# The first layer's last convolution on two row halves of TensorE, x pieces kept in SBUF, stores moved to GpSimd's queue, and an earlier start of the second scan chunk

## The chip, the cores and the metric

The kernel runs on 1 core of one Trainium2 chip. The metric is the device time of one execution in microseconds (us). The kernel before was run three times: 11592.89 us is the median, from 11590.45 to 11595.39. The engines are named as in the profile: PE (TensorE), DVE (VectorE), ACT (ScalarE), POOL (GpSimd) and SP (SyncE, which here only issues DMAs).

## The reference

Two pre-activation layers with residuals on x of shape (4, 192, 128, 128), all in float32:

```python
x = x + _L0_conv_ref(_gn(x), ...)   # layer0 in the code
x = x + _L1_conv_ref(_gn(x), ...)   # layer1 in the code: the selective scan
```

`_gn` is a group norm over 32 groups of 6 channels. The first layer, cut to what matters:

```python
x1 = c1x1(gn(x), conv1_w)                    # 192 -> 48 channels: x_0, x_05, x_1, 16 each
Fre = frft2d(x_05, 0.5)                      # fractional Fourier transform
mag_out, pha_out = ...                       # 3x3 and 1x1 convolutions on |Fre| and angle(Fre)
ifrft = abs(frft2d(mag_out * exp(1j*pha_out), -0.5))
fre = rfft2(x_1)                             # the same with an ordinary 2D FFT and a 1x1 convolution
x_1o = irfft2(...)
y = c1x1(concat([c1x1(x_0, conv_0_w) + conv_0_b, ifrft, x_1o]), conv2_w)   # 48 -> 192 channels
```

The second layer turns each image into 16384 tokens of 192 channels, applies a layer norm, an input projection to 2 x 384, a causal convolution of 4 taps and SiLU, forms dt, B and C, runs the recurrence `h = h * exp(dt*A) + dt*u*B` with 16 states for each of 384 channels, gates `sum(h*C) + u*D` with SiLU(z) and projects back to 192 channels.

## The kernel before, in words

**`layer0`** takes the four images one after another. An image is cut into 16 pieces of 8 rows: a piece (tile `xt`) is 96 partitions x 2 x 1024 floats, 768 KB, loaded by `load` (L186, SP's queue) into a pool of 6 buffers. Three generators do the work of an image.

- `analysis` reads all 16 pieces for the group statistics (`bn`, L192, DVE), folds them into the weights `w1r`, and reads all 16 pieces a second time for the first convolution (L278). L278 works on two column halves of PE: output channels of the first 512 pixels go to PSUM partitions 0 to 63, those of the second 512 to 64 to 127. ACT evacuates (L282) and stores the 48 channels into the DRAM tensor `d1` (L288, ACT's queue).
- `branches` (26 steps) loads `d1`'s upper 32 channels (L294), does the two-sided transforms as matmuls (`spectrum`, L214 and L224), turns them into magnitude and phase (`_polar`: DVE, ACT, and one POOL add at L78), and passes every change of layout through DRAM: stores of `dmag`, `dp` (L303), `dh` (L310), `df` (L372), `di` (L392), `dimg` (L453) and loads of the same, all on SP's queue. The squares of the inverse transform are added on POOL (L421).
- `synthesis` is the last convolution with the residual. Per piece it loads `xt` again, 16 channels of `d1`, 32 of `dimg` and a row of ones into `cat` (49 rows x 1024; L464, L465, L466, SP's queue, two buffers), multiplies the 49 rows by `w2x` (L471: four matmuls of 49 rows, 96 columns and 512 elements), adds the result to `xt` (L475, DVE), takes the statistics for the second layer (L192) and stores the piece into `xmid` (L477, POOL's queue, software descriptors).

At L488 to L497 the generators are interleaved: each step of `branches(b)` is followed by one or two steps of `analysis(b + 1)` (`ahead`) and, at even steps, by one of `synthesis(b - 1)` (`behind`); what is left of both is run out before the next image. `synthesis(3)`, of the last image, runs alone. Within `layer0` a planner with assumed costs decides the order of instructions on each engine; an engine's order is then fixed, and an instruction that waits holds back all that follow on its engine or queue.

**`layer1`** has 128 chunks of 512 tokens; its order is written out by hand. `front(n)` is a generator of 34 steps for what comes ahead of the scan: layer norm (L610 to L658), input projection (L664), convolution (L682), SiLU (L690, L694), x projection (L726), the store of B and C to DRAM (`dbc`, L731), dt (L740, L745), dtu (L749, POOL) and the rest of the projection. `load_bc` broadcasts a pair of states' B and C from `dbc` to 128 partitions (`bc`, 1 MB each, 8 per chunk, L774). The main loop has 24 groups (3 channel tiles x 8 pairs of states) per chunk: scans on DVE (L869) with factors from ACT (L800) and inputs from DVE (L820), POOL (L828) or PE (L855), products with C on POOL (L882), sums on PE (L895). Steps of `front(n + 1)` and `front(n + 2)` run within the loop. Before the loop `front(0)` runs to its end, then the eight `load_bc` of chunk 0 and the first factors are issued, and then 10 steps of `front(1)`.

Of the kernel before, what the change touches and what calls it, by code (L numbers as in the profile page):

```python
# [121 lines left out]
def layer0(tc, x, xmid, st2, w):  # L122

    nc = tc.nc
    B = x.shape[0]
    with ExitStack() as ctx:
        def pool(name, bufs, **kw):
            return ctx.enter_context(tc.tile_pool(name=name, bufs=bufs, **kw))

        cp = pool("l0c", 1)  # L130
        dram = pool("l0d", 2, space=DRAM)
        xp = pool("l0x", 6)
        sp = pool("l0s", 2)
        imp = pool("l0i", 2)
        zp = pool("l0z", 2)
# [13 lines left out]
        ri_cat, ri_out = const("ri_cat"), const("ri_out")  # L149


        w2x = cp.tile([3 * NC + 1, C], F32, name="w2x")
        nc.sync.dma_start(out=w2x[NC : 3 * NC, :], in_=w["w2T"][NC:, :])
        w20, c0 = cp.tile([NC, C], F32, name="w20"), const("c0")
        nc.sync.dma_start(out=w20, in_=w["w2T"][0:NC, :])
        ps = psA.tile([128, 512], F32, name="ps")
        nc.tensor.matmul(ps[0 : NC + 1, 0:C], c0, w20, start=True, stop=True)
        folded = cp.tile([NC + 1, C], F32, name="folded")
        nc.vector.tensor_copy(folded, ps[0 : NC + 1, 0:C])
        nc.sync.dma_start(out=w2x[0:NC, :], in_=folded[0:NC, :])  # L160
        nc.sync.dma_start(out=w2x[3 * NC :, :], in_=folded[NC:, :])
        half_pi = cp.tile([128, 1], F32, name="half_pi")
        nc.vector.memset(half_pi, math.pi / 2)

# [4 lines left out]
        dmag = []  # L169
        zrow = cp.tile([1, S], F32, name="zrow")  # L170
        nc.vector.memset(zrow, 0.0)
        orow = cp.tile([1, PIECE], F32, name="orow")
        nc.vector.memset(orow, 1.0)
        for i in range(min(2, B)):
            d = dram.tile([NC * S + 2, S], F32, name=f"dmag{i}", bufs=1)
            nc.sync.dma_start(out=d[0:1, :], in_=zrow)
# [6 lines left out]
        def load(b, p):  # L183
            xt = xp.tile([CH, 2, PIECE], F32, name="xt")
            src = x[b].rearrange("c h w -> c (h w)")[:, p * PIECE : (p + 1) * PIECE]
            nc.sync.dma_start(out=xt, in_=split(src))  # L186
            return xt

        def bn(st, p, xt):
            for t in range(2):  # L190
                for q in range(PIECE // 512):
                    nc.vector.bn_stats(  # L192
                        st[:, t, p * (PIECE // 512) + q, :], xt[:, t, q * 512 : (q + 1) * 512]
                    )
# [52 lines left out]
        def analysis(b, got):  # L247


            st = sp.tile([CH, 2, NPIECE * (PIECE // 512), 6], F32, name="st")  # L250
            for p in range(NPIECE):
                bn(st, p, load(b, p))
                yield
            gst = sp.tile([CH, 2, 2], F32, name="gst")
            bn_done(st, gst)

            w1r = sp.tile([CH, 2, 128], F32, name="w1r")
            for t in range(2):  # L260
                nc.vector.tensor_scalar(w1r[:, t, :], w1T[:, t, :], gst[:, t, 1:2], None, ALU.mult)
            ps = psA.tile([128, 512], F32, name="ps")
            for t in range(2):
                nc.tensor.matmul(
                    ps[:, 0:1], w1r[:, t, :], gst[:, t, 0:1], start=t == 0, stop=t == 1
                )
            b1 = sp.tile([128, 1], F32, name="b1")
            nc.vector.tensor_scalar(b1, ps[:, 0:1], -1.0, None, ALU.mult)
            d1 = got["d1"] = dram.tile([3 * NC, S * S], F32, name="d1")
            for p in range(NPIECE):  # L270
                xt = load(b, p)
                if p % 2 == 0:
                    x1 = sp.tile([128, 2, 512], F32, name="x1")
                ps = psA.tile([128, 512], F32, name="ps")
                for t in range(2):
                    for q in range(2):
                        half = slice(64 * q, 64 * (q + 1))
                        nc.tensor.matmul(  # L278
                            ps[half], w1r[:, t, half], xt[:, t, q * 512 : (q + 1) * 512],
                            start=t == 0, stop=t == 1,  # L280
                        )
                nc.scalar.activation(x1[:, p % 2, :], ps, AF.Identity, bias=b1)  # L282
                if p % 2 == 1:
                    at = d1[:, (p - 1) * PIECE : (p + 1) * PIECE].rearrange(
                        "c (e q f) -> q c e f", e=2, q=2
                    )
                    for q in range(2):
                        nc.scalar.dma_start(out=at[q], in_=x1[64 * q : 64 * q + 3 * NC])  # L288
                yield

        def branches(b, got):
# [6 lines left out]
            for half in range(2):  # L298
                mag, pha = yield from spectrum(
                    xT, 0, fr2[:, 0, :], fr2, S, (2 * half, 2 * half + 1)  # L300
                )
                for src, dst in ((mag, dm[1 : NC * S + 1, :]), (pha, dp)):
                    nc.sync.dma_start(  # L303
                        out=by_row(dst, 8 * half, 8), in_=src.rearrange("k (c l) -> k c l", c=8)
                    )

            dh = [dram.tile([NC * S, L], F32, name=f"dh{i}") for i in range(2)]
            polar = yield from spectrum(xT, NC, rf1, rf2, L, range(4))
            for src, dst in zip(polar, dh):
                nc.sync.dma_start(  # L310
                    out=by_row(dst, 0, NC), in_=src.rearrange("k (c l) -> k c l", c=NC)
                )

# [20 lines left out]
            for half in range(2):  # L334
# [34 lines left out]
                    )  # L369
                    yield  # L370
                for src, dst in zip(_from_polar(nc, up, half_pi, mo, po, n), df):
                    nc.sync.dma_start(  # L372
                        out=dst.rearrange("(p r) l -> p (r l)", r=16)[:, half * n : (half + 1) * n],
                        in_=src,
                    )
# [13 lines left out]
                inner.append(t)  # L389
                yield  # L390
            for src, dst in zip(_from_polar(nc, up, half_pi, *inner, n), di):
                nc.sync.dma_start(out=dst.rearrange("(p r) l -> p (r l)", r=16), in_=src)  # L392


            img = imp.tile([128, 2 * NC, S], F32, name="img")
# [54 lines left out]
                )  # L450
                yield
            dimg = dram.tile([2 * NC, S, S], F32, name="dimg")
            nc.sync.dma_start(out=dimg.rearrange("c h w -> h c w"), in_=img)  # L453
            got.update(dimg=dimg)

        def synthesis(b, got):

            d1, dimg = got["d1"], got["dimg"].rearrange("c h w -> c (h w)")
            st = sp.tile([CH, 2, NPIECE * (PIECE // 512), 6], F32, name="st2")
            for p in range(NPIECE):  # L460
                xt = load(b, p)
                cat = qp.tile([3 * NC + 1, PIECE], F32, name="cat", bufs=2)
                at = slice(p * PIECE, (p + 1) * PIECE)
                nc.sync.dma_start(out=cat[0:NC, :], in_=d1[0:NC, at])  # L464
                nc.sync.dma_start(out=cat[NC : 3 * NC, :], in_=dimg[:, at])  # L465
                nc.sync.dma_start(out=cat[3 * NC :, :], in_=orow)  # L466
                for q in range(PIECE // 512):
                    at = slice(q * 512, (q + 1) * 512)
                    pr = psB.tile([128, 2, 512], F32, name="pr")
                    for t in range(2):  # L470
                        nc.tensor.matmul(  # L471
                            pr[0:CH, t, :], w2x[:, t * CH : (t + 1) * CH], cat[:, at],
                            start=True, stop=True,
                        )
                    nc.vector.tensor_add(xt[:, :, at], xt[:, :, at], pr[0:CH])  # L475
                bn(st, p, xt)
                nc.gpsimd.dma_start(  # L477
                    out=split(xmid[b][:, p * PIECE : (p + 1) * PIECE]), in_=xt
                )
                yield  # L480
            bn_done(st, st2[:, b])
# [6 lines left out]
        behind = iter(())  # L488
        for b in range(B):
            ahead = analysis(b + 1, got[b + 1]) if b + 1 < B else iter(())  # L490
            for i, _ in enumerate(branches(b, got[b])):
                next(ahead, None)
                next(ahead if i % 2 else behind, None)
            for rest in (behind, ahead):
                for _ in rest:
                    pass
            behind = synthesis(b, got[b])  # L497
        for _ in behind:
            pass

# [3 lines left out]
def layer1(tc, xmid, out, st2, w, n_tok=S * S):  # L504
# [12 lines left out]
    with ExitStack() as ctx:  # L517
# [253 lines left out]
        def load_bc(i, sg):  # L771

            t = bcp.tile([128, 2, G, T], F32, name="bc")
            nc.sync.dma_start(  # L774
                out=t, in_=got[i]["dbc"][:, sg * G : (sg + 1) * G, :].partition_broadcast(128)
            )
            got[i]["bc", sg] = t
# [184 lines left out]
        def go_on(parts, part):  # L962

            for f in parts[part]:
                got_on = next(f, None)
                if got_on is not None:
                    parts[got_on].append(f)

        with tc.manual_schedule():
            for i in range(min(2, total)):  # L970
                load_x(i)
            for _ in front(0):
                pass
            for sg in range(NG):
                load_bc(0, sg)
            dtu_copy(0, 0)
            inputs(*order[1])
            for at in range(AHEAD):
# [3 lines left out]
            decay_there(2)  # L982


            start_front(1)
            for _ in range(NGR - FRONT):
                parts = {MID: [], LATE: []}
                step(fronts, parts)
                go_on(parts, MID)
                go_on(parts, LATE)  # L990
            tails = []
            for pos, (n, k) in enumerate(order):
                j, sg = divmod(k, NG)
# [193 lines left out]
```

## Time and profile before

| | before |
|---|---|
| median of 3 runs | 11592.89 us |
| the profiled execution | 11590.68 us |
| its span, first to last instruction | 11588.6 us |
| granted PE clock, mean | 0.931 |
| DVE, POOL, PE, ACT busy | 93%, 87%, 85%, 74% of the span |
| `layer0`, to the last statistics (L192) | 0 to 1440 us |
| before the first scan (L869) | 1440 to 1523 us |
| scans | 1523 to 11588 us |

The span is what the profiler saw; the 2.1 us beside it lie around it. In a timeline line the first number is the start in us from the span's start, the second the duration; in brackets stands how long the engine had been idle and what released it. "x8" counts records, and each of these float32 matmuls leaves two. In a table by windows each engine has its busy time and the number of records, then follow the granted PE clock as a fraction, the mean busy share of the 16 DMA engines and GB/s.

### The profile page before, as it was taken

The numbers are of one execution on the slowest core, as the hardware profiler recorded it, in microseconds if no ns is written. First come the engines' busy times: TensorE is split into PE (matmuls) and PEld (weight loads), VectorE is DVE, ScalarE is ACT, GpSimd is POOL, SyncE is SP. The second block draws the span as 40 slices with busy tenths as digits, with TensorE's granted clock in tenths as the row PEclk, the third lists the DMA queues.
The fourth block names the chain that finished last, engine by engine and source line by source line (L and its number), as shares of the span: only waits on it lengthen the run. The fifth ranks groups of instructions, "written<-read, shape, count | busy, mean of one in ns | idle before, by whom it ended". The sixth has DMA issues, their size and how long they took to land.

```text
span 11588.6 us, 153548 instructions
## 1 busy us (share of the span) xinstructions
PE 9794.3 (85%) x50570; PEld 6612.4 (57%) x50570; DVE 10751.8 (93%) x11584; ACT 8608.4 (74%) x14436; POOL 10072.1 (87%) x4598
## 2 busy tenths in 40 slices
PE   4777888888888888888888888888888888888887
PEld 2444356655656665655665665665655666566565
DVE  5565679999999999999999999999999999999999
ACT  2322168888888888888888888888888888888886
POOL 0000079999999999999999999999999999999999
PEclk8888789999999999999999999999999999999998
DMA  8787734434434434433433443443443343344343
GB/s 209 203 221 202 195 99 126 120 108 127 126 103 128 126 107 122 126 112 117 126 118 110 126 125 104 127 127 104 124 126 111 118 126 116 113 126 123 106 127 97
DMA packets 1339384, 1494.09 MB, mean 129 GB/s; under 512 B 903474, under 2 KB 954359, under 8 KB 1338071
## 3 DMA queue, kind: packets, MB, share of 16 engines
q1 hardware_dynamic: 1318102, 1421.34, 42.5%
q0 software_dynamic: 13312, 50.34, 1.4%
q10 hardware_dynamic: 7168, 12.59, 0.3%
q8 instruction: 398, 6.52, 0.2%
q14 instruction: 404, 3.30, 0.1%
HBM read 1325.19 MB, written 155.32 MB: 128 GB/s over the span
## 4 chain that ended last, share of the span: by engine, by line
DVE 32%; ACT 23%; PE 22%; issue 14%; POOL 6%; DMA 2%; DVEq 0%; SPq 0%; POOLq 0%; ACTq 0%
DVE h L869 23%; DVE op L820 7%; PE py L895 6%; ACT da L800 6%; POOL hc L882 4%; ACT op L800 4%; ACT L800 2%; ACT dbT L844 2%; PE py L909 2%; PE ps L664 2%; PE pr L471 2%; ACT dt L745 1%; POOL db L828 1%; PE ps L682 1%; PE op L855 1%
## 5 line engine op out<-in xcount | busy, mean ns | idle before, releaser
L882 POOL TENSOR_TENSOR hc<-h,bc 128x1024 f32<-128x1024 f32 x3072 | 7195.2, 2374 | 95.7 <-DVE h L869 93.7
L869 DVE TENSOR_TENSOR_SCAN h<-da,carry,op 128x512 f32<-128x512 f32 x3968 | 4932.9, 1263 | 0.0
L895 PE MATMUL py<-ident,hc 128*128 128x128 f32 x24576 | 3346.1, 283 | 604.5 <-ACT yt L904 368.3
L895 PEld LDWEIGHTS py<-ident,hc 128*128 128x128 f32 x24576 | 2941.5, 147 | 1589.7 <-issue 701.4
L800 ACT ACTIVATE da<-dt,c_A_log 128x512 f32<-128x512 f32 x4096 | 2828.1, 722 | 626.3 <-DVE h L869 620.1
L869 DVE TENSOR_TENSOR_SCAN h<-op,carry,db 128x512 f32<-128x512 f32 x1984 | 2508.4, 1264 | 86.0 <-issue 82.0
L828 POOL TENSOR_TENSOR db<-dtu,bc 128x1024 f32<-128x1024 f32 x1024 | 2425.6, 2369 | 6.3 <-DMA bc<-dbc 6.3
L820 DVE TENSOR_TENSOR op<-dp,bc 128x512 f32<-128x512 f32 x3328 | 2232.6, 671 | 32.1 <-ACT dp L783 32.1
L800 ACT ACTIVATE op<-dt,c_A_log 128x512 f32<-128x512 f32 x2048 | 1400.3, 689 | 896.4 <-DVE h L869 894.0
L664 PE MATMUL ps<-s,c_wiT 96*128 96x512 f32 x3072 | 1452.3, 595 | 2.6 <-DVE s L658 2.6
L682 PE MATMUL ps<-xs,dcw 128*128 128x512 f32 x3072 | 1424.4, 593 | 0.4 <-ACT xs L677 0.4
L933 PE MATMUL ps<-yg,c_woT 128*96 128x512 f32 x1536 | 712.1, 600 | 186.5 <-DVE xm L939 186.5
L800 ACT ACT_TABLE_LOAD x636 | 816.0, 1283 | 11.6 <-DVE h L869 0.3
L844 ACT ACTIVATE dbT<-ps,bT 128x128 f32<-128x128 f32 x3072 | 822.0, 371 | 0.0
L682 PEld LDWEIGHTS ps<-xs,dcw 128*128 128x128 f32 x3072 | 533.5, 190 | 432.3 <-issue 431.7
L664 PEld LDWEIGHTS ps<-s,c_wiT 96*128 96x128 f32 x3072 | 526.1, 191 | 379.4 <-issue 376.1
L477 POOL DMA_DIRECT2D xmid<-xt x64 | 42.6, 666 | 789.8 <-DVE xt L475 783.2
L933 PEld LDWEIGHTS ps<-yg,c_woT 128*96 128x96 f32 x1536 | 241.0, 163 | 553.8 <-issue 307.6
L633 PE MATMUL ps<-ones,xs 96*128 96x1 f32 x2048 | 292.7, 273 | 287.2 <-ACT dt L745 282.3
L909 PE MATMUL py<-ddp,u 128*128 128x128 f32 x3072 | 520.1, 326 | 0.0
L749 POOL TENSOR_TENSOR dtu<-dt,u 128x512 f32<-128x512 f32 x384 | 478.6, 1284 | 29.6 <-ACT dt L745 29.6
L909 PEld LDWEIGHTS py<-ddp,u 128*128 128x128 f32 x3072 | 487.6, 241 | 0.0
(172 smaller groups left out, 10247.2 us busy)
## 6 DMA issues: line engine op xcount, KB each, us to landing
bc<-dbc SPq DMA_DIRECT2D x1024, 1024.0 KB, 5.9
xt<-in_x SPq DMA_DIRECT2D x192, 768.0 KB, 9.6
xmid<-xt POOLq DMA_DIRECT2D x64, 768.0 KB, 7.1
xm<-xmid SPq DMA_DIRECT2D x128, 384.0 KB, 3.5
carry<-h SPq DMA_DIRECT2D x3072, 1.0 KB, 1.9
out<-xm SPq DMA_DIRECT2D x128, 384.0 KB, 3.3
d<-x ACTq DMA_DIRECT2D x64, 192.0 KB, 6.9
df<-u SPq DMA_DIRECT2D x16, 512.0 KB, 4.9
```

The costliest lines, as they stand in the source:

```text
L664: nc.tensor.matmul(pp, wiT[:, t, m * 128 : (m + 1) * 128], s[:, t, :], start=t == 0, stop=t == 1)
L682: nc.tensor.matmul(pc, dcw[:, j, k, :], xs[:, j, k : k + T], start=k == 0, stop=k == 3)
L749: nc.gpsimd.tensor_tensor(dtu[j], dt[j], u[j], ALU.mult)
L800: nc.scalar.activation(da, got[n]["dt"][j], AF.Exp, scale=A[:, j, st : st + 1])
L820: nc.vector.tensor_tensor(dbs[s], g["dp"], g["bc", k % NG][:, 0, q, :], ALU.mult)
L828: nc.gpsimd.tensor_tensor(db, _bc(g["dtu"][j], 1, G), g["bc", sg][:, 0], ALU.mult)
L844: nc.scalar.activation(t[:, blk, :], g["tu", j][:, blk, :], AF.Identity, scale=g["bT"][:, blk, q : q + 1])
L869: nc.vector.tensor_tensor_scan(h[:, q, :], das.pop(s), dbs.pop(s) if db is None else db[:, q, :], 0.0 if ch == 0 else g["before"][:, j, st ...
L882: nc.gpsimd.tensor_tensor(hc, h, g["bc", sg][:, 1], ALU.mult)
L895: nc.tensor.matmul(py[:, blk, :], hc[:, q, blk * 128 : (blk + 1) * 128], ident, start=first, stop=sg == NG - 1 and q == G - 1 and blk == T ...
L909: nc.tensor.matmul(got[n]["py", j][:, blk, :], got[n]["u"][j][:, blk * 128 : (blk + 1) * 128], ddp[:, j, :], start=False, stop=False, skip ...
L933: nc.tensor.matmul(po[0:CH], woT[:, j, t * CH : (t + 1) * CH], g["yg", j], start=j == 0, stop=j == NJ - 1,)
```

## The change

Six edits in `layer0` and one in `layer1`.

1. `cat` becomes two fixed tiles of 128 rows x 512, set to one at the start: rows 0 to 48 hold the first 512 pixels of a piece, rows 64 to 112 the second; `w2x` is held twice, likewise. The row of ones is no longer loaded. The loop turns around: for each of the two halves of the output channels, one matmul on rows 0 to 48 and one on rows 64 to 112, into the two banks of one PSUM tile, then one add.
2. `cat` is loaded by four DMAs per piece from POOL's queue instead of three from SP's.
3. `analysis` keeps the last four pieces of the statistics pass and starts the first convolution with them: 12 loads there instead of 16. The pool of `xt` has 7 buffers instead of 6.
4. The stores of `dmag`, `dp`, `dh`, `df`, `di` and `dimg` go to POOL's queue instead of SP's.
5. During the last image `synthesis(2)` gets a step at every step of `branches(3)`, not at every second one.
6. After step 18 of `branches(3)` the first four pieces of `synthesis(3)` are loaded.
7. Before the main loop of `layer1`, the 10 steps of `front(1)` go between steps 18 to 27 of `front(0)`, and the eight `load_bc` follow step 25 of it.

```diff
-        xp = pool("l0x", 6)
+        xp = pool("l0x", 7)
...
+        cats = [cp.tile([128, 512], F32, name=f"cat{i}") for i in range(2)]
+        for cat in cats:
+            nc.vector.memset(cat, 1.0)
...
             for p in range(NPIECE):
-                bn(st, p, load(b, p))
+                xt = load(b, p)
+                if p >= NPIECE - KEEP:
+                    kept[p] = xt
+                bn(st, p, xt)
                 yield
...
-            for p in range(NPIECE):
-                xt = load(b, p)
+            for p in (*range(NPIECE - KEEP, NPIECE), *range(NPIECE - KEEP)):
+                xt = kept.pop(p, None) or load(b, p)
...
-                    nc.sync.dma_start(
+                    nc.gpsimd.dma_start(
                         out=by_row(dst, 8 * half, 8), in_=src.rearrange("k (c l) -> k c l", c=8)
                     )
...
-            nc.sync.dma_start(out=dimg.rearrange("c h w -> h c w"), in_=img)
+            nc.gpsimd.dma_start(out=dimg.rearrange("c h w -> h c w"), in_=img)
...
-                xt = load(b, p)
-                cat = qp.tile([3 * NC + 1, PIECE], F32, name="cat", bufs=2)
-                at = slice(p * PIECE, (p + 1) * PIECE)
-                nc.sync.dma_start(out=cat[0:NC, :], in_=d1[0:NC, at])
-                nc.sync.dma_start(out=cat[NC : 3 * NC, :], in_=dimg[:, at])
-                nc.sync.dma_start(out=cat[3 * NC :, :], in_=orow)
-                for q in range(PIECE // 512):
-                    at = slice(q * 512, (q + 1) * 512)
+                xt = early[p] if p < len(early) else load(b, p)
+                cat = cats[p % 2]
+                for q in range(2):
+                    at = slice(p * PIECE + q * 512, p * PIECE + (q + 1) * 512)
+                    nc.gpsimd.dma_start(out=cat[64 * q : 64 * q + NC, :], in_=d1[0:NC, at])
+                    nc.gpsimd.dma_start(out=cat[64 * q + NC : 64 * q + 3 * NC, :], in_=dimg[:, at])
+                for t in range(2):
                     pr = psB.tile([128, 2, 512], F32, name="pr")
-                    for t in range(2):
+                    for q in range(2):
+                        rows = slice(64 * q, 64 * q + 3 * NC + 1)
                         nc.tensor.matmul(
-                            pr[0:CH, t, :], w2x[:, t * CH : (t + 1) * CH], cat[:, at],
+                            pr[0:CH, q, :], w2x[rows, t * CH : (t + 1) * CH], cat[rows, :],
                             start=True, stop=True,
                         )
-                    nc.vector.tensor_add(xt[:, :, at], xt[:, :, at], pr[0:CH])
+                    nc.vector.tensor_add(
+                        xt[:, t, :], xt[:, t, :], pr[0:CH].rearrange("p q f -> p (q f)")
+                    )
...
             for i, _ in enumerate(branches(b, got[b])):
                 next(ahead, None)
-                next(ahead if i % 2 else behind, None)
+                next(ahead if i % 2 and b < B - 1 else behind, None)
+                if b == B - 1 and i == LOADS:
+                    early = [load(b, p) for p in range(KEEP)]
...
-            for _ in front(0):
-                pass
-            for sg in range(NG):
-                load_bc(0, sg)
+            first = [front(0)]
+            for i in range(2 * NGR - FRONT):
+                if i == NGR - 6:
+                    start_front(1)
+                once(first)
+                if NGR - 6 <= i < 2 * NGR - FRONT - 6:
+                    once(fronts)
+                if i == NGR + 1:
+                    for sg in range(NG):
+                        load_bc(0, sg)
...
-            start_front(1)
-            for _ in range(NGR - FRONT):
-                parts = {MID: [], LATE: []}
-                step(fronts, parts)
-                go_on(parts, MID)
-                go_on(parts, LATE)
```

`KEEP` is 4, `LOADS` 18, `NGR` 24, `FRONT` 14, `B` 4. `once(works)` is the four removed lines at the end as a helper: one step of each generator and its later parts.

## The prediction

> **What bounds the kernel now.** I first read busy time by stage, cut where the images begin (each row: PE, PEld, DVE, ACT, POOL busy, then granted clock, DMA share, GB/s).
>
> ```profile
> 0.00:126.00 126.00, 39.75 (x138) 12.80 (x138) 51.42 (x90) 12.04 (x18) 0.20 (x4) 0.95 0.96 261
> 126.00:389.00 263.00, 176.31 (x685) 108.51 (x686) 148.33 (x183) 88.93 (x121) 14.15 (x11) 0.82 0.79 200
> 389.00:730.00 341.00, 264.44 (x837) 139.49 (x835) 192.46 (x229) 90.04 (x123) 24.55 (x27) 0.81 0.78 205
> 730.00:1075.00 345.00, 260.68 (x848) 139.82 (x849) 211.69 (x271) 91.16 (x126) 24.24 (x28) 0.80 0.82 217
> 1075.00:1320.00 245.00, 208.42 (x677) 119.06 (x676) 169.04 (x188) 75.29 (x101) 23.79 (x27) 0.86 0.62 168
> 1320.00:1445.00 125.00, 110.54 (x133) 36.50 (x132) 81.70 (x110) 0.41 (x2) 10.56 (x18) 0.50 0.72 211
> ```
>
> The first 126 us (statistics and first convolution of image 0) are DMA's, at 0.96 of its time. From 126 to 1320 us nothing is full: PE about 76%, DMA about 0.76, DVE about 60%. From 1320 us, the last image's `synthesis`, PE is at it without a break and at half clock. After 1523 us DVE and POOL are full (98%, 99%) up to the end, and no instruction of the main loop changes: each us by which the first scan comes earlier is one off the end.
>
> The chain of waits from 126 to 1320 us says what the mixed stages hang on, and the timeline what the last one does:
>
> ```profile
> by line: issue 23.1%; PE pr L471 8.0%; PE ps L278 6.6%; DVE u L87 5.5%; PE ps L415 5.2%; PE ps L244 4.8%; PE ps L407 4.5%; DMA xt<-in_x 4.1%; DVE st L192 3.7%; PE ps L348 3.4%; DMA u<-df 3.3%; PE ps L437 2.6%; DVE xt L475 2.5%; DVE u L112 2
> ```
> ```profile
> 1327.65 109.51 PE L471 MATMUL pr<-cat,w2x 49*96 49x512 f32 x128 [7.58 <-issue]
> ...
> 1375.76 1.22 DVE L475 TENSOR_TENSOR xt<-xt,pr 96x1024 f32<-96x1024 f32 x1 [1.38 <-PE pr L471]
> ...
> 1376.90 1.87 DVE L192 BATCH_NORM_STATS2 st<-xt 96x6 f32<-96x512 f32 x3
> ...
> 1377.27 0.63 POOL L477 DMA_DIRECT2D xmid<-xt  x1 [6.20 <-DVE xt L475]
> ```
>
> So L471 holds 8.0% of 1194 us = 95.5 us of that chain, and the x loads 4.1% = 49 us. In the last stage a piece takes 109.5/16 = 6.84 us, DVE waits for PE, POOL for DVE. A piece asks of DVE two adds of 1.22 and four statistics of 0.62, 4.9 us.
>
> Last, how the scan starts:
>
> ```profile
> 1494.51 0.31 SPq L731 DMA_DIRECT2D dbc<-xd  x1
> ...
> 1506.56 2.35 POOL L828 TENSOR_TENSOR db<-dtu,bc 128x1024 f32<-128x1024 f32 x1 [6.28 <-DMA bc<-dbc]
> ...
> 1512.53 1.22 DVE L620 SCALAR_TENSOR_TENSOR s<-ps,s 96x1024 f32<-96x1024 f32 x1 [7.67 <-PE ps L617]
> ...
> 1521.80 1.22 DVE L658 TENSOR_TENSOR s<-s,ps 96x1024 f32<-96x1024 f32 x1 [2.83 <-PE ps L653]
> 1522.94 2.32 DVE L869 TENSOR_TENSOR_SCAN h<-da,op 128x512 f32<-128x512 f32 x2
> ```
>
> The scan's operands are there by about 1507 us; it stands on DVE behind `front(1)` until 1522.94.
>
> **What the Trainium skill says.** "TensorE: Matmul & The Clock Gate", Part 3: matmuls on different row groups run at once in the array. The trace shows it for column halves, not for row halves:
>
> ```profile
> 341.33 1.94 PE L278 MATMUL ps<-xt,w1r 96*64 96x512 f32 x8
> ...
> 429.16 1.95 PE L471 MATMUL pr<-cat,w2x 49*96 49x512 f32 x4
> ```
>
> Eight records in halves take as long as four without. Part 1 there: PE is at half rate until it has been busy; the trace agrees on the half rate (0.50), but L471 stays there through 109 busy us. "TensorEngine Tiling (Array Packing)", Key Properties: a change of tiling mode drains PE; no row shows such a cost, and I take none. "DMA: Bandwidth & Descriptors", "Issuing engines are not separate DMA queues": all queues share the same 16 engines, and another queue saves only issue time. So moving stores brings no bandwidth. In its section "SWDGE vs HWDGE vs iDMA": GpSimd's descriptors are computed by software; the trace agrees in that POOL is 0.63 us at a 768 KB store of 192 rows where SP is about 0.33 us at a load of the same size.
>
> **The change, part by part** (against the profiled 11590.7 us).
>
> *a. Image 0.* Its second pass reads 12 pieces instead of 16. Loads follow each other every 3.07 us (the statistics start at 25.70, 28.79, 31.87), so 12.3 us less DMA; four of the seven buffers are held when the convolution begins, so the queue then runs dry for about 2 us. Late next is PE, 1.94 us a piece. **−10** (−12 to −5).
>
> *b. x loads of images 1 to 3.* Kept pieces take away 12 x 3.07 = 37 us of DMA time, and SP's queue, where loads stood 198 us behind `cat` loads that wait for L471, now holds only loads. All this works at the chain's 49 us of x loads. DVE and PE are late next: half, **−25** (−49 to 0).
>
> *c. L471 up to 1320 us.* Two row halves at once halve 95.5 us: **−48** (−60 with the slower clock relieved, 0 if halves don't run at once). The adds (2 x 1.22 us a piece, as before) and bn are hidden as now.
>
> *d. Stores on POOL.* The row price is unknown. From below: 0 beyond SP's. POOL's extra 0.3 us over 192 rows: 1.6 ns a row. From above: the fastest `xmid` store lands 4.6 us after issue, 1.5 us more than its 3.07 us of data: 8 ns a row. I take 1.6. On an image's path lie half of `dmag` (1024 rows) and of `df` (128): 1.8 us, four times, 7; `dimg` (4096 rows, 6.6 us) for images 0 to 2 lies half beside the next image, 10. **+17** (0 to +85 at 8 ns). POOL's adds L78, L421 wait in the same queue; POOL is 5 to 10% busy there and ACT's other work covers that.
>
> *e. The last stage.* PE needs two pairs of 1.71 us at half clock (3.4 us a piece), DVE 4.9. But the built order puts POOL's DMAs so that in every three pieces two `cat` loads stand behind the `xmid` store of an earlier piece, which waits for its add. A link is: two pairs 3.4, add 1.2, store issue 0.65, load issue 0.65, landing L; two links per three pieces: 2 x (5.9 + L). Before, three pieces took 20.5 us, so the two are equal at L = 4.35. The load lies behind 768 KB in the same queue:
>
> ```profile
> DMA to landing us min/median/max: 4.6/7.1/12.6
> ```
>
> (`xmid` from issue). Less 1.3 us of issues, L is 3.3 alone, 5.8 beside x loads; I take 4.5. Then, from the landing of `dimg`: first matmul at 4.2, add ends 8.8, piece 2 at 14.6, piece 3 at 25.0, piece 15 after four rounds of 20.8 at 108.2, end at 114.7; before it was 1440.2 − 1325.1 = 115.1. So 0, plus `dimg`'s rows, 6.6. **+7** (−28 to +30). Steps 5 and 6 bring the four loads forward into time when DMA is at 0.62; in the last stage they were hidden behind PE anyway. Step 5 packs `synthesis(2)` into 16 steps; 0.
>
> *f. Start of the scan.* `front(1)`'s steps go into gaps of `front(0)` and cost PE and ACT there: L617, L633, L653 took 3.7 + 3.6 + 2.0 us at half clock, part of it hidden: +8 on `front(0)` up to `dbc`, 1502.5; the second `bc` landed 12 us after `dbc`'s issue, so 1514.5, and the first scan comes at about 1514, late next being `bc`. 1522.9 − 1514 = 9; **−8** (−15 to 0). The eight `load_bc` pass no waiting DMA on SP.
>
> Sum: −10 − 25 − 48 + 17 + 7 − 8 = −67: 11523.7 in the profiled execution. The median stands 2.2 above that one before: 11525.9, rounded to **11525**.
>
> **The rivals.**
> 1. *More comes*: c at −60, x loads at −49, a −12, POOL's rows nothing (+0), the last stage with L = 3.3 (−12) and half of its links' pair time gone because the clock rises (−17), f −12: −162, 11430. For it: PE at 0.80 clock in 76% of its time; against: DVE is 60% full and its reciprocals (L87, 6.6 us) stand alone in the chain.
> 2. *Hidden anyway*: DVE and round trips through DRAM set the pace from 126 to 1320 us: a −5, b 0, c −12, d +17, e +7, f −8: −1, 11590. For it: the share "issue", 23.1%.
> 3. *Row halves don't run at once*: c 0; a link is then 9.3 + L, three pieces 27.6 us, the last stage +38 and 6.6: −10 − 25 + 17 + 45 − 8 = +19, 11612. Against: column halves do.
> 4. *Slower*: POOL's price per row. With a, b, c, f unchanged (−91) and 14.7 us for each ns (d 10.6, `dimg` at the end 4.1), the change loses above 6.2 ns a row; at 8 ns it is −91 + 118 = +27, 11620. For it: nothing here shows POOL with more than 192 rows; against: 0.63 us for 192.
>
> **How the numbers follow.** About 0.2% (23 us) is what a measurement of this kernel can tell from no change. Chances: forecast 0.50, rival 1 0.20, 2 0.12, 3 0.05, 4 0.13. Faster: 0.48 + 0.20 + 0.03 = 0.71; same: 0.02 + 0.08 + 0.02 + 0.02 = 0.14; slower: 0.01 + 0.03 + 0.11 = 0.15. The range leaves out half of rivals 1 and 4: 11430 to 11620; the forecast's own, from its terms, is 11470 to 11570.
>
> **What the profile after would show.** L471 as pairs, its records starting two by two, and its share of the chain to 1320 us halved; image 0's L294 load about 10 us earlier; `xmid` rounds of about 7 us in the last stage with PE idle between pieces; POOL's rows for `dimg` near 7 us; first scan 9 us sooner relative to the last statistics. Wrong would be: L471 pairs one after the other, `dimg` rows above 20 us, or stages from 126 to 1320 us as long as before with L471 halved.

## The result, and the profile after

The changed kernel takes 11539.27 us (median of 4 runs, 11533.06 to 11541.51) against 11591.67 us of the kernel before on the same chip: ratio 0.9957, 95% interval 0.9944 to 0.9969. The profiled execution took 11541.51 us, its span is 11539.7 us; the span was 11588.6 us before.

Busy time by stage, cut at the last `xT` load of image 0's analysis, the four `dimg` stores, the last statistics and the first scan (columns: stretch, length, then PE, PEld, DVE, ACT, POOL busy, granted clock, DMA share, GB/s). First the kernel before, at its own such points, then the changed one:

```profile
126.00:398.60 272.60, 185.19 (x728) 115.74 (x728) 153.85 (x192) 92.44 (x127) 14.15 (x11) 0.83 0.79 200
398.60:704.80 306.20, 244.00 (x774) 128.73 (x775) 174.96 (x205) 86.53 (x117) 22.94 (x24) 0.82 0.76 200
704.80:1040.50 335.70, 252.19 (x829) 134.15 (x828) 207.64 (x262) 89.79 (x123) 23.97 (x27) 0.82 0.84 220
1040.50:1310.20 269.70, 224.40 (x705) 126.67 (x704) 176.64 (x200) 76.66 (x104) 24.75 (x29) 0.83 0.63 171
1310.20:1440.20 130.00, 113.66 (x139) 37.30 (x137) 86.95 (x113) 0.20 (x1) 10.99 (x18) 0.51 0.74 217
```
```profile
124.30:392.60 268.30, 182.76 (x720) 114.72 (x721) 154.45 (x192) 90.64 (x124) 23.20 (x23) 0.84 0.75 195
392.60:695.80 303.20, 219.34 (x801) 119.03 (x800) 194.52 (x236) 88.23 (x120) 68.55 (x102) 0.83 0.76 213
695.80:1001.90 306.10, 234.18 (x828) 128.57 (x828) 195.09 (x243) 89.59 (x123) 68.44 (x105) 0.81 0.78 218
1001.90:1264.60 262.70, 184.53 (x696) 113.21 (x696) 173.54 (x202) 77.06 (x105) 68.84 (x106) 0.84 0.61 173
1264.60:1402.30 137.70, 89.63 (x128) 25.42 (x128) 76.14 (x97) 0.00 (x0) 41.62 (x77) 0.52 0.62 176
```

PE's busy time falls by 25, 18 and 40 us in the stages of images 1 to 3, but the stages only by 3, 30 and 7 us. In the last one PE falls by 24 us and the stage grows by 7.7; POOL is busy four times as long. The chain of waits of that last stage in the changed kernel says why:

```profile
by line: PE pr L484 31.0%; DMA cat<-dimg 30.2%; DVE xt L488 12.1%; DMA dimg<-img 7.8%; issue 7.7%; DVE st L201 7.5%; POOL cat L479 2.2%; POOL xmid L492 1.8%; POOL cat L478 1.3%; POOLq L479 0.0%
...
1292.92 1.23 DVE xt L488
...
1294.43 0.42 POOL xmid L492
...
1295.08 9.24 DMA cat<-dimg
...
1304.45 3.71 PE pr L484 x4
```

Add, `xmid` store, landing of a `cat` load, pairs of matmuls, and round again: the convolution (L484, L471 before) is 31% of the chain, the landing `cat` loads another 30%. The start of the scan came nearer: its last statistics end at 1402.3, and the first scan stands at 1475.44, 73.2 us later; it was 82.7 us before. From the first scan to the end nothing changed (10064.3 us, 10065.7 before).

### The profile page after: what moved, and what is told of

It reads as the page before. It is cut to its first block, busy times and chain, and to the rows that moved or that the text cites. A ratio compares the mean times of both kernels' runs of the same rounds, so it can differ in the third digit from the quotient of the medians.

```text
span 11539.7 us, 153703 instructions
## 1 busy us (share of the span) xinstructions
PE 9667.5 (84%) x50570; PEld 6555.8 (57%) x50570; DVE 10749.4 (93%) x11585; ACT 8606.8 (75%) x14435; POOL 10247.7 (89%) x4906
## 4 chain that ended last, share of the span: by engine, by line
DVE 31%; ACT 24%; PE 16%; issue 11%; POOL 5%; DMA 2%; DVEq 0%; POOLq 0%; SPq 0%; ACTq 0%
DVE h L887 23%; DVE op L838 7%; ACT da L818 6%; PE py L913 6%; ACT op L818 5%; POOL hc L900 4%; ACT L818 2%; ACT dbT L862 2%; PE py L927 2%; PE ps L682 2%; ACT dt L763 2%; ACT L763 1%; PE op L873 1%; PE ps L671 1%; DMA carry<-h 1%
## 5 line engine op out<-in xcount | busy, mean ns | idle before, releaser
L201 DVE BATCH_NORM_STATS2 st<-xt 96x6 f32<-96x512 f32 x512 | 321.4, 678 | 176.4 <-DMA xt<-in_x 175.4
## 6 DMA issues: line engine op xcount, KB each, us to landing
d<-x ACTq DMA_DIRECT2D x64, 192.0 KB, 7.7
```

## The experiments

Spans of one profiled execution, cut as above: to image 0's `dimg` store, the stages of images 1, 2 and 3, the last `synthesis`, the start of the scan. The ratio is that of the times to the kernel before.

| kernel | ratio (95%) | to dimg 0 | 1 | 2 | 3 | last | start |
|---|---|---|---|---|---|---|---|
| before | 1 | 398.7 | 306.1 | 335.8 | 269.7 | 129.9 | 82.7 |
| changed | 0.9957 (0.9944–0.9969) | 392.7 | 303.2 | 306.1 | 262.7 | 137.7 | 73.2 |
| e4_xmid_act | 0.9926 (0.9914–0.9939) | 392.6 | 302.1 | 303.5 | 260.5 | 100.4 | 74.3 |
| e7_cat_sp | 0.9906 (0.9892–0.9919) | 396.3 | 291.5 | 289.3 | 266.1 | 97.9 | 74.3 |
| b1_cat_pool | 1.0050 (1.0036–1.0064) | 402.9 | 324.8 | 331.0 | 262.4 | 185.8 | 82.2 |
| b2_halves_only | 0.9933 (0.9919–0.9946) | 400.4 | 295.8 | 319.1 | 247.1 | 101.9 | 83.1 |
| e1_all_rows | 0.9950 (0.9938–0.9963) | 389.0 | 301.4 | 307.2 | 261.8 | 126.0 | 73.5 |
| e9_sp_all_rows | 0.9920 (0.9906–0.9933) | 390.7 | 298.1 | 292.4 | 260.4 | 108.0 | 73.4 |
| e3_sp_stores | 0.9958 (0.9944–0.9971) | 392.1 | 304.5 | 309.0 | 263.0 | 131.9 | 72.3 |
| e10_sp_all_sp | 0.9931 (0.9919–0.9944) | 391.0 | 299.8 | 320.4 | 263.1 | 96.3 | 73.5 |
| e2_no_kept | 0.9962 (0.9949–0.9974) | 395.1 | 298.3 | 304.7 | 261.9 | 134.7 | 75.3 |
| e8_six_x | 0.9971 (0.9960–0.9982) | 397.2 | 306.5 | 305.3 | 260.5 | 133.9 | 73.1 |
| e5_x1_eight | 0.9956 (0.9943–0.9968) | 388.6 | 303.4 | 304.0 | 262.8 | 134.2 | 72.9 |
| e11_even_steps | 0.9898 (0.9882–0.9915) | 395.3 | 297.1 | 291.0 | 252.5 | 97.9 | 73.2 |

Two things limit what such a table can say. Executions of one kernel spread over 6 to 19 us, and each row of stages is one of them: e4 has the changed kernel's text for the first three images, and PE and DVE work in the same order, yet it is 6 us shorter between the first and the last `dimg` store. And an edit also moves the order that the planner gives the engines of `layer0`. Going by their tiles, about 100 of DVE's 1059 instructions stand elsewhere between the changed kernel and e7, and between e7 and e10; of those compared, only e4 leaves both PE and DVE as they were. No run moves the order alone, so it is an untested rival in what follows, except for e4.

My first theory was that the row halves (edit 1) and the freed SP queue (edit 2) had made the gain. The rivals: the halves are hidden; POOL's order takes back what they give.

**GpSimd's queue (edit 2).** e4, on the changed kernel:

```
-                nc.gpsimd.dma_start(
+                out_q = nc.scalar if b == B - 1 else nc.gpsimd
+                out_q.dma_start(
                     out=split(xmid[b][:, p * PIECE : (p + 1) * PIECE]), in_=xt
```

> The changed kernel with the 16 xmid stores of the last image on ACT's queue instead of GpSimd's; the first three images as in the changed kernel. Theory (the last stage's 137.6 us are POOL's order: a cat load stands behind the xmid store of an earlier piece, which waits for its add): the cat loads then wait only for the cat tile of two pieces ago, a piece takes about 5 to 6 us instead of 7, and the stage falls to 100 to 120 us: 11505 to 11522 in all. Rival (PE at half clock, or DMA with x loads, xmid stores and cat loads together at 0.72 share, bounds the stage anyway): within 5 us of 11539.

The last stage fell from 137.7 to 100.4 us, no other stage moved by over 3 us: POOL's order set the last stage, as the theory said (the median, 11500.67 us, is even 4 us below its range). Next, the loads themselves:

```
-nc.gpsimd.dma_start(out=cat[64 * q : 64 * q + NC, :], in_=d1[0:NC, at])
-nc.gpsimd.dma_start(out=cat[64 * q + NC : 64 * q + 3 * NC, :], in_=dimg[:, at])
+nc.sync.dma_start(...)   both
```

> The changed kernel with the four cat loads of a piece issued by SP again instead of GpSimd. Theory (what the stages of images 1 to 3 gained is that SP no longer keeps x loads behind cat loads that wait for L484; the row halves gave nothing there): 20 to 40 us more between image 0's and the last image's dimg stores; the last stage changes too, since a cat load no longer stands behind an xmid store: -20 to +5 us; in all 11535 to 11580. Rival (the gain came from the seventh x buffer, the kept pieces or the halves): the stages before the last dimg store within 8 us of the changed kernel's.

The theory fell, in the opposite direction: the stages of images 1 to 3 together did not get longer but 25 us shorter, and the last one 40 us shorter. The whole is 60 us less than the changed kernel. SP's own waits from 396 to 1243 us, of the changed kernel and of this one (line, what it waited for: us, times, longest):

```profile
SPq L195 <- DMA xmid<-xt: 561.1, 49, 84.1
SPq L195 <- PE ps L291: 88.6, 24, 10.1
```
```profile
SPq L195 <- DMA xmid<-xt: 219.5, 34, 24.2
SPq L478 <- PE pr L484: 191.8, 47, 14.3
SPq L195 <- PE ps L291: 53.8, 18, 8.2
```

The wait of x loads behind `cat` loads (192 us) did leave SP, but POOL then has it ("POOL cat L478 <- PE pr L484", 192.0 us from 124 to 1264), and SP's x loads wait 342 us more than in e7 for the buffer that an `xmid` store has to free. But that wait is no measure of the loss: between the same two stores it is 134 us in the kernel before, 364 in e3, which takes as long as the changed kernel, and 144 in e10, which takes 29 us longer than e7. Nor are the `xmid` stores late in POOL's queue: the traces have the 48 stores of images 0 to 2 starting on average 0.55 us after the last add of their piece in the changed kernel, and 0.38 us in e7. So the 25 us are measured, and how POOL's queue, or the order that comes with it, costs them is not shown. The same part alone, on the kernel before:

```
-nc.sync.dma_start(out=cat[...], ...)     three loads
+nc.gpsimd.dma_start(out=cat[...], ...)
```

> The kernel before with one part of the change alone: its three cat loads of a piece on GpSimd's queue; six x buffers, no kept pieces, one row group, stores on SP. Theory (edit 2 made the gain): 30 to 45 us less between image 0's and the last image's dimg stores than before, while the last stage gets 10 to 25 us longer (a cat load behind an xmid store in GpSimd's queue, pairs one after the other): 11560 to 11590. Rival (it was the seventh buffer or the halves): no gain up to the last dimg store, 11595 to 11620 in all.

58 us slower in the median. In the profiled execution it is 64: 11 before the last `dimg` store, so no gain there at all, against the theory, and 56 in the last stage, beyond the rival's range too. The chain of that stage shows the round bare:

```profile
1381.25 13.95 PE pr L471 x16
...
1395.22 1.23 DVE xt L475
...
1396.74 0.48 POOL xmid L477
...
1397.38 4.89 DMA cat<-orow
...
1402.51 13.95 PE pr L471 x16
```

Two pieces take 21.3 us, 13.95 of PE and 7.3 of add, store issue, load issue and landing; in the kernel before, PE went through two pieces in 13.7.

**The row halves (edit 1).** Alone, on the kernel before (SP's queue, six buffers):

```
-    cat = qp.tile([3 * NC + 1, PIECE], F32, name="cat", bufs=2)
-    (three loads; per q, per t: pr[0:CH, t, :], w2x, cat[:, at])
+    cat = cats[p % 2]
+    (four loads on nc.sync; per t, per q: pr[0:CH, q, :], w2x[rows], cat[rows])
```

> The kernel before with edit 1 alone: row halves, two constant cat tiles, four cat loads a piece, issued by SP as before; six x buffers, no kept pieces, stores on SP, old start of the scan. Theory (with cat loads on SP the row halves do pay: the last stage of the kernel before was PE's, at 6.84 us a piece, and becomes DVE's, 4.9 us a piece): the last stage falls from 130 to 98 to 105 us. In the stages of images 1 to 3 they free the cat tiles, on which SP's queue stands, sooner: 10 to 30 us less. In all 11525 to 11555. Rival (what the stages of images 1 to 3 gained is the stores on GpSimd's queue and the buffers): these stages within 5 us of before, 11555 to 11565.

77 us less than before, more than expected: 50 in the stages of images 1 to 3 (10, 17, 23) and 28 in the last. Edit 1 alone beats the whole change by 30 us of span (the intervals of the ratios just touch). Its chain up to the last `dimg` store has half of the last convolution's time, 4.2% of 1132 us = 47.5 us (L476 is L471 here), where the kernel before had 95.5:

```profile
by line: issue 22.7%; PE ps L283 6.8%; PE ps L249 5.7%; DMA u<-df 5.4%; PE ps L420 4.9%; DVE u L87 4.6%; PE ps L412 4.6%; PE pr L476 4.2%; PE ps L353 4.0%; DVE st L197 3.1%; DMA xt<-in_x 3.1%; PE ps L442 2.7%; DMA cat<-dimg 2.6%; DVE u L112
```

Edit 1 holds more than the halves, though: `cat` in two fixed tiles, no row of ones to load, and the loop turned around. No run takes these apart. Then the concurrency of the halves taken away from the changed kernel:

```
-    rows = slice(64 * q, 64 * q + 3 * NC + 1)
-    pr[0:CH, q, :], w2x[rows, t * CH : (t + 1) * CH], cat[rows, :],
+    pr[0:CH, q, :], w2z[q][:, t * CH : (t + 1) * CH], cat,     (w2z[q]: 128 rows, zero outside half q)
```

> The changed kernel with the two row halves' concurrency taken away and nothing else: each of the four matmuls of a piece reads all 128 rows of cat, with zero weights for the rows that are not its half, so that no two can run at once; loads, adds, stores and order are as in the changed kernel. Theory (row halves are what the stages of images 1 to 3 gained, and the last stage hangs on them through its links): the time rises from 11539 by 25 to 60 us, most of it between image 0's and the last image's dimg stores (140 to 220 us less PE room in three stages), and the last stage grows from 137.6 to about 160 us, as two links per three pieces each take 3.4 us more. Rival (the concurrency is hidden, and the gain came from the queues and the kept pieces): under 10 us more in all.

No loss, as the rival had it: the interval overlaps that of the changed kernel. The last stage is even 11.6 us shorter, but there POOL's order is not that of the changed kernel: it goes in rounds of two pieces with two `xmid` stores, instead of three with three. So that stage does not test the halves alone. The timelines of one piece in the last stage, first of the changed kernel, then of this one:

```profile
1304.45 7.09 PE L484 MATMUL pr<-cat,w2x 49*96 49x512 f32 x12 [5.29 <-DMA cat<-dimg]
...
1306.47 1.22 DVE L488 TENSOR_TENSOR xt<-xt,pr 96x1024 f32<-96x1024 f32 x1 [9.96 <-PE pr L484]
...
1308.18 1.22 DVE L488 TENSOR_TENSOR xt<-xt,pr 96x1024 f32<-96x1024 f32 x1 [0.49 <-PE pr L484]
```
```profile
1273.35 9.57 PE L484 MATMUL pr<-cat,w2z 128*96 128x512 f32 x16 [15.30 <-DMA cat<-dimg]
...
1277.09 1.22 DVE L488 TENSOR_TENSOR xt<-xt,pr 96x1024 f32<-96x1024 f32 x1 [18.30 <-PE pr L484]
...
1278.47 0.16 PEld L484 LDWEIGHTS pr<-cat,w2z 128*96 128x96 f32 x1 [0.49 <-issue]
1278.90 0.16 PEld L484 LDWEIGHTS pr<-cat,w2z 128*96 128x96 f32 x1 [0.27 <-issue]
1279.33 0.16 PEld L484 LDWEIGHTS pr<-cat,w2z 128*96 128x96 f32 x1 [0.27 <-issue]
1279.53 1.22 DVE L488 TENSOR_TENSOR xt<-xt,pr 96x1024 f32<-96x1024 f32 x1 [0.50 <-PE pr L484]
```

With halves, half a piece is at the add 2.0 us after its first matmul, and the other half 1.71 us later: they do run at once (in the kernel before, the four products of a piece took 6.84 us, 1.71 each, at the same clock). Over 128 rows the first half takes 3.7 us, one product after the other; but 5 us after the start the weight loads come every 0.43 us instead of every 0.85: the clock has risen, and a piece costs the same 3.4 us of PE (8 x 0.43) as the pairs at half clock. The granted clock of the last stage was 0.79 here and 0.52 with halves. Once more with `cat` loads on SP:

> The version with cat loads on SP, and with the halves' concurrency taken away again by matmuls over all 128 rows with zero weights. Theory (a piece of four 128-row products, one after the other, runs at a granted clock near 0.8 to 1.0 and takes 3.4 to 4.5 us of PE, less than DVE's 4.9; the 49 rows of the kernel before were bound because they stayed at half clock): the last stage within 5 us of 97.9, and the whole within 8 us of 11480. Rival (concurrency is what took PE off the path in the last stage): last stage 110 to 130 us, 11492 to 11515.

Between the two: the last stage is 108.0 us (97.9 with halves), its clock 0.84, and the median is 12 us higher, with intervals that overlap. From image 0's to the last `dimg` store it is 851 us against 847. What the last convolution takes of PE between these stores, in the kernel before, in e7 and in e9 (sums over the three stages: their length, then PE and PEld busy in L471 or L484):

```profile
sum 911.60, PE 218.63 PEld 62.44; mean PE 72.88 PEld 20.81
```
```profile
sum 846.80, PE 135.67 PEld 34.43; mean PE 45.22 PEld 11.48
```
```profile
sum 851.00, PE 195.98 PEld 63.71; mean PE 65.33 PEld 21.24
```

With the halves taken away it is nearly back at what it was, and yet these stages do not grow. What falls instead is the rest of PE's work, from 501 us in e7 to 468 (502 before), at a clock of 0.87 to 0.91 where e7 has 0.84 to 0.85. So in the stages of images 1 to 3 of these runs the halves at once are not needed. In the last stage they seem to help: DVE waits 33 us for PE in e9, 23 in e7 (its order in the last five pieces differs too). When PE has waited for a `cat` load, its weight loads come every 0.85 us again (from 1312.56 to 1316.82 in e9), and products over 128 rows, one after the other, then take up to 3.7 us for half a piece.

**The stores on POOL (edit 4).** `nc.gpsimd` back to `nc.sync` at L316, L323, L385, L405 and L466, in the changed kernel:

> The changed kernel with the stores of dmag, dp, dh, df, di and dimg issued by SP again, as before; the cat loads stay on GpSimd's queue. Theory (a POOL store costs 0.49 us and 0.3 ns a row, nothing like 1.6 to 8 ns, so POOL's price is next to nothing, but on SP a store that waits for its data holds back the x loads behind it): 5 to 20 us more than 11539, in the stages of images 1 to 3. Rival 1 (the prediction's price of POOL's rows, 17 us): 10 to 17 us less. Rival 2 (the queue of a store does not matter): within 3 us.

No difference in the time (the same ratio to 0.0001), as rival 2 had it, against both the theory and the prediction's 17 us. POOL's rows in the changed kernel (count, busy in all, mean ns) show the price:

```profile
L385 POOL DMA_DIRECT2D df<-u x16 | 8.8, 549 | 72.4 <-DVE u L117 63.8 <-DVE u L118 4.2 <-issue 3.1
...
L316 POOL DMA_DIRECT2D dmag<-u x8 | 7.3, 914 | 9.8 <-ACT u L79 9.8
L466 POOL DMA_DIRECT2D dimg<-img x4 | 7.0, 1740 | 75.6 <-issue 75.6
```

128 rows take 549 ns, 1024 take 914, 4096 take 1740: near 0.5 us and 0.3 ns a row. With the `cat` loads on SP it is otherwise:

> The version with cat loads on SP and the stores of dmag, dp, dh, df, di and dimg on SP as well. Theory (the stores wait for spectra and hold back x and cat loads behind them on SP, which their move to GpSimd's queue ended): 15 to 45 us more between the first and the last dimg store than with the stores on GpSimd (396.3 to 1243.1), last stage as there: 11495 to 11525. Rival (a store's queue does not matter, as with the cat loads on GpSimd's queue): within 5 us of 11480.

As the theory said: 29 us more in the span than with stores on POOL (11508.4, 11479.9), and 36 more from the first to the last `dimg` store, 31 of them in image 2's stage. What SP waits for there, at the stores' lines among others:

```profile
SPq L478 <- PE pr L484: 76.5, 10, 16.3
...
SPq L316 <- ACT u L79: 12.2, 2, 9.1
...
SPq L385 <- DVE u L118: 7.5, 2, 6.2
SPq L405 <- DVE u L117: 6.4, 1, 6.4
```

In these three lines the stores hold 26 us of SP's time in that stage, ahead of x and `cat` loads. In these runs, then, edit 4 pays only where SP's queue also carries the `cat` loads, which edit 2 took off it.

**Kept pieces, buffers, image 0 (edit 3).**

```
-            for p in (*range(NPIECE - KEEP, NPIECE), *range(NPIECE - KEEP)):
+            for p in range(NPIECE):                     (and nothing is put into kept)
```

> The changed kernel without kept pieces: analysis loads all 16 pieces twice, in order, as before; the early loads of the last image stay. Theory (the kept pieces took DMA time from image 0, where the d1 store then came late next, and hold four of seven buffers in the other images, which SP then waits for): 2 us more for image 0's first xT load (126 against 124.3) and between 5 us less and 5 us more in the stages of images 1 to 3; the whole within 8 us of 11539. Rival (the prediction's terms a and b: kept pieces are worth their DMA time): 20 to 35 us more.

Within what can be told apart from the changed kernel, as the theory said of the whole: 5 us more in the median, 8 less in the profiled span. The first `xT` load comes 4.6 us later (128.85), but the eight kernels here whose image 0 has the changed kernel's text have it anywhere from 123.75 to 130.34. With six buffers besides:

> The changed kernel without kept pieces in analysis (as in the run without kept pieces) and with six x buffers instead of seven. Theory (the seventh buffer is worth little once SP's queue holds only loads and stands nowhere behind matmuls): 0 to 8 us more than the run without kept pieces (span 11531.6, last dimg store 1260.0). Rival (the seventh buffer made the gain of images 1 to 3): 25 to 45 us more, most of it before the last dimg store.

9 us more in the span, just above the expected range; the intervals overlap. Last, what is late in image 0:

```
+                if p % 2 == 0 and b == 0:
+                    x1 = roomy[:, (p + 4) % 8 // 2]     (eight x1 in two img tiles; b > 0 as before)
```

> The changed kernel with eight x1 buffers instead of two in image 0's second pass (they lie in the img tiles, which are free then). Theory (after the kept pieces the d1 store came late next in image 0: ACT waits 3.5 to 5.5 us per pair of pieces for a d1 store to free x1): the first xT load comes 7 to 10 us earlier, at 114 to 117 instead of 124.3, and so does everything up to the last dimg store: 11529 to 11533. Rival (x loads or PE hold image 0's second pass anyway, or a later stage takes it back): the first xT load within 3 us of 124.3 or the whole within 3 us of 11539.

The theory fell and the rival held: the first `xT` load came at 121.88 instead of 124.28. ACT's timeline of the changed kernel, then PE's with eight buffers:

```profile
93.86 1.27 ACT L295 ACTIVATE x<-ps,b 128x512 f32<-128x512 f32 x2 [3.97 <-DMA d<-x]
...
98.67 1.26 ACT L295 ACTIVATE x<-ps,b 128x512 f32<-128x512 f32 x2 [3.54 <-DMA d<-x]
```
```profile
99.08 1.94 PE L296 MATMUL ps<-xt,w1r 96*64 96x512 f32 x8 [1.13 <-DMA xt<-in_x]
102.12 1.94 PE L296 MATMUL ps<-xt,w1r 96*64 96x512 f32 x8 [1.10 <-DMA xt<-in_x]
```

The wait for the `d1` store is gone, and PE waits in its place for x pieces, which come 3.04 us apart here (3.07 in the first pass, which is DMA's).

**The last image's steps (edits 5 and 6),** undone in the version with `cat` loads on SP:

```
-                next(ahead if i % 2 and b < B - 1 else behind, None)
-                if b == B - 1 and i == LOADS: early = [load(b, p) for p in range(KEEP)]
+                next(ahead if i % 2 else behind, None)
```

> The version with cat loads on SP (span 11479.9), with edits 5 and 6 undone: beside the last image's branches, synthesis of image 2 takes a step only at every second step, as before, and no x pieces are loaded early. Theory (from edit 1 alone against all edits but 2 and 4, image 3's stage 247 against 263 us and the last stage 102 against 96: packing synthesis(2) and the early loads into the last image's branches costs more there than the last stage gets back): the last image's stage 10 to 18 us less than 266, the last stage 2 to 8 us more than 97.9; in all 11465 to 11477. Rival (that difference comes from the kept pieces or from noise of the order): within 4 us of 11480.

Image 3's stage is 13.6 us shorter, within what was expected. The last stage is unchanged (97.9 both), where 2 to 8 us more had been expected: edits 5 and 6 together brought it nothing. The span is 8.5 us less (11471.4). The median is 11471.96 us, the best of all, 67 us below the changed kernel; but its interval and that of e7 overlap, so the 8 us rest on one profile each.

## Why the prediction was right, and where it was not

The forecast was 11525 us, the time is 11539; the span changed by −49 us, where −67 stood. That the sum came so near is luck in good part, for no rung of the way there came as its terms said. The ladder of spans: before 11588.6; edit 1 alone 11510.0 (−79, where c has −48 and the last stage none); with edits 3, 5, 6 and 7 too 11508.4 (−2, where a and f alone have −18); with edit 4 11479.9 (−29, where d has +17); with edit 2, the changed kernel, 11539.7 (+60, where b has a gain and e +7). The effects depend on this order, as edit 4 shows.

*a. Image 0, −10*: mis-sized. The eight kernels whose image 0 has the changed kernel's text have the first `xT` load 3 us earlier on average than the five without kept pieces (125.6 against 128.8), and the `dimg` store 6 us (392.5 against 398.8). "Late next is PE" was wrong: the `d1` store (ACT waits 2.2 to 5.5 us a pair for it) and, with that gone, x loads again. The second pass also stores `d1` over the same DMA.

*b. x loads, −25*: this step failed. "SP's queue ... now holds only loads. All this works at the chain's 49 us": moving the `cat` loads costs 25 us in these stages instead (847 to 872 us from the first to the last `dimg` store, e7 against changed), and kept pieces bring nothing that can be told apart. I priced the queue that the `cat` loads left, and not the one they joined: the wait for the convolution, 198 us on SP before, is 192 us on POOL after. How that comes to 25 us is open.

*c. Row halves, −48*: edit 1 alone gave 50 us up to the last `dimg` store, the size that I took, and halved the convolution's share of the chain. But that this share is what the stages gained does not follow: in e9 the convolution has 196 us of PE again, near the 219 of before, and these stages are within 4 us of e7's. PE's work as a whole is 57 us less than before there, at the higher clock, and 84 less in e7. Whether that or the rest of edit 1 made the 50 us is open, and the match in size may be luck.

*d. Stores on POOL, +17*: wrong in size and sign. I took 1.6 ns a row from one store of 192 rows, all of the excess over SP put on rows; most of it is the fixed 0.5 us. At 0.3 ns a row, `dimg` is 1.7 us and not 6.6. Rival 4, which needed 6.2 ns, is out. The use of the move, SP's queue set free, stood in the sum only within b's "now holds only loads", not as a worth of its own: 29 us if the `cat` loads stay on SP, and 0 here.

*e. Last stage, +7*: measured +7.7, and the mechanism, a `cat` load behind an `xmid` store, is shown by e4. Landings in the changed kernel's chain are 2.0 to 9.2 us, around the 4.5 taken. That the number fits so closely is luck: 6.6 of the 7 were `dimg`'s rows. And +7 was a balance of −32 from the halves (e7 against before) and +40 from POOL's order: I worked out the equality with "before" and did not ask what the stage would be without POOL, although the bottom of its range, −28, lies near that.

*f. Start of the scan, −8*: 82.7 to 73.2, −9.5. No run undoes edit 7 alone; but the three kernels with the old start have 82.2 to 83.1 us, the eleven with the new one 72.3 to 75.3. Late next is ACT, not `bc` as I had it:

```profile
1470.96 2.34 POOL L846 TENSOR_TENSOR db<-dtu,bc 128x1024 f32<-128x1024 f32 x1 [4.48 <-DMA bc<-dbc]
...
1472.78 0.59 ACT L801 COPY dp<-dtu 128x512 f32<-128x512 f32 x1
...
1473.39 1.28 ACT L818 ACT_TABLE_LOAD   x1
1473.40 1.30 DVE L838 TENSOR_TENSOR op<-dp,bc 128x512 f32<-128x512 f32 x2 [11.18 <-ACT dp L801]
...
1475.44 2.33 DVE L887 TENSOR_TENSOR_SCAN h<-da,op 128x512 f32<-128x512 f32 x2 [0.74 <-ACT da L818]
```

`bc` has landed by 1471; DVE has waited 11 us for ACT's copy `dp`, and the scan then for `da` behind a table load.

Of the signs I named, pairs starting two by two, `xmid` rounds with PE idle between, and the scan's 9 us came; image 0's 10 us and `dimg`'s 7 us on POOL did not. The halved share of the chain came with edit 1 alone; in the changed kernel's trace the chain cannot be followed back so far. Of the signs of being wrong one came in part: the stages of images 1 and 3 are only 3 and 7 us shorter, with the convolution at 135 us of PE instead of 219.

Open: by what way edit 1 gains in the stages of images 1 to 3 and why so differently (10, 17, 23 us for the same edit), how edit 2 costs 25 us there, and how much of all this is the planner's order.

## What to carry to other kernels

Moving DMAs to another queue moves their waits too: write down what stands behind them in the new queue. Here the store that ends one round (it waits for an add) stood ahead of the load that begins a later one, and that cost the last stage 37 us (e4); keep such a pair apart. When a sum gives "no change" for a stage with two opposite parts, test the parts alone: one of them may be worth keeping without the other. A long wait on a queue is not yet a loss. And where a planner sets the order, compare the order of two kernels before a difference between them is put down to the edit.

## What was not expected of the hardware

- GpSimd's DMA issue: 549 ns at 128 rows, 914 at 1024, 1740 at 4096. The Trainium skill, "DMA: Bandwidth & Descriptors", "SWDGE vs HWDGE vs iDMA", says that descriptors are computed there by software; the trace shows that for these stores this comes to 0.3 ns a row.
- The granted clock of the last stage went with the rows of a product: 0.50 to 0.55 with 49-row products, in halves at once as well as alone, 0.79 and 0.84 when the same sums went over 128 rows. It is not how long PE is busy: that is 70 of 98 us in e7 (0.51) and 68 of 108 in e9 (0.84). Among other work of PE, 49-row products ran at the full rate (in the kernel before four records took 1.95 us at 429 us, 3.4 in the last stage). "TensorE: Matmul & The Clock Gate", Part 1, has full rate after about 3.4 us of busy PE; the 128-row runs agree (about 5 us), the last stage of the kernel before does not (half rate through 109.5 us). The cause is open.
